# Adjacency loads on another queue, trial sums rearranged, and output tiles opened behind the last search

## The chip, the core and the metric

The kernel runs on one core of a Trainium2 chip. A core has a matrix engine (TensorE, PE in the profile), a vector engine (VectorE, DVE), a scalar engine (ScalarE, ACT), a general-purpose engine (GpSimd, POOL) and a queue that mostly issues DMAs (SyncE, SP). ScalarE and GpSimd can issue DMAs too. Each engine works through its own instructions in order, and they wait for each other by semaphores. The metric is the device time of one execution in microseconds (us).

## The reference, cut to what matters

Two layers over N = 3327 nodes with 256 features. `adj` is a 3327 × 3327 matrix of zeros and ones, about four ones in a row.

```python
# layer 0
Wh  = h @ W
e   = leaky_relu(Wh @ a[:F] + (Wh @ a[F:]).T, 0.2)
att = softmax(where(adj > 0, e, -9e15), axis=1)
x   = layernorm(x + GRU(att @ Wh, x))
# layer 1, two steps; S is adj
R = (S + eye) / rowsum
for n in range(2):
    A  = top_p_attention(Xa, W1, W2, W3)   # softmax of (q k^T); of each row the largest
                                           # probabilities that sum to 0.9 are kept
    Xf = R @ Xf
    Xa = A @ Xa
    Z  = Z + Xf @ U1[n].T + Xa @ U2[n].T
h = X + Z
x = layernorm(x + layernorm(h) * ln_g + ln_b)
```

Everything is in 32-bit floats.

## The kernel before

The rows are cut into 26 tiles of 128 (the last has 127). The work has four stages in the profile: layer 0's projection (0 to about 65 us), layer 0's attention and gates, tile by tile (to about 300), layer 1's first step (about 330 to 960) and second step (about 1000 to 1570), and a tail (to the end at 1846.6).

**Layer 0.** Each tile's adjacency rows are loaded into one of three buffers (`load_adj`, two DMAs of 1248 and 415.5 KB). The vector engine finds the ones of each row (`neighbours`, L819). When it has finished a tile, its number plus three is put on the list `wanted`, since that buffer is free. `advance` counts phases, takes one tile at a time from `wanted`, and issues its load on SP; it also drives the generators `tile(t)`, one opened every 6 phases. Meanwhile `project(t)` computes x W for every tile on PE, ACT copies it out and stores it to a table in DRAM (`whx`). In `tile(t)` GpSimd prepares small vectors (`d1`, `half`, `square`), gathers five times 128 rows of `whx` at the neighbours' numbers (L613), and the other engines turn them into attention and gates. The loads of tiles 1 and 2 go on ACT's queue inside the projection; behind the projection ACT asks for the gates' weights (`whh`, `wih`, 1.54 MB together).

In layer 0 the order on PE, ACT, DVE and GpSimd is the order in which the program is written; in layer 1 the same holds for PE, ACT and DVE, while GpSimd's and SP's orders are chosen by a scheduler.

**Layer 1's step.** For each tile: logits and their exponentials, a search for the threshold that keeps 0.9 of the mass (DVE), a mask, and the product with Xa on PE (`product`, with seven slots into which other work of neighbouring tiles is put).

**Extra tiles.** Rows whose list of candidates was too short in step 2 are put aside (`put_aside_2` stores their data to `left_over` in DRAM at L1531) and searched again in three extra tiles, h0, h1 and h2 (HARD = 3). For each extra tile k: `hard_load` reads the rows' data and gathers their features; `hard_q` computes the query on PE and ACT; `hard_exp` computes the 3327 probabilities. Then an upper bound `top` on the threshold is lowered by trial sums: for f in CUTS = 1/16, 1/4, 1/2, 0.707, 0.841, 0.917, the mass above f × top is summed, and top is multiplied by f when it is less than the wanted mass. A trial sum is done either on ACT (`coarse_bound`: four passes over the probabilities with L1602, and seven small instructions on GpSimd, L1608 to L1617), or on DVE (`bound` with `kept_sum`, L1341: one pass with two inputs from on-chip memory and three small instructions; its comparison at L1632 reads `thr`, which GpSimd makes at L1626). h0 has two cuts on ACT and four on DVE; h1 and h2 have three on each (COARSE = 3). `hard` is the search itself, on DVE (L1644 to L1673 and on); `hard_end` the product and output terms on PE; `hard_store` scatters the rows into the output at L1708.

**Output tiles.** `tile_end(t)`, a generator of eight steps, loads a tile's intermediate rows, transposes them on PE (L1181), sums 16 products and the input on PE (L1440, L1492), copies the sum out on ACT (L1448) and normalizes it twice with statistics on DVE (L1383, L1385), a power on GpSimd (L1386, L1387) and three instructions on ACT.

**The tail's order.** `ends` writes it. DVE's program is the searches of h0, h1, h2, one behind the other. Each `yield` of a search runs `more()`: one step of the queue of the extra tiles' own work (h2's query and exponentials, then the ends of h0, h1, h2), one `tick`, and up to two steps of a coarse bound. A tick opens one new output tile and takes every open one a step further. Since a search has 8 yields and the trial sums in front of h1's and h2's search have three each, there are 30 ticks in the searches.

Of the kernel before, what the change touches and what calls it, by code (L numbers as in the profile page):

```python
# [17 lines left out]
N = 3327  # L18
# [629 lines left out]
class Layer0:  # L648
# [186 lines left out]
    def tile(self, t):  # L835
# [23 lines left out]
        d16 = self.small("d16", f"d16_{t}", dtype=BF16)  # L859
        nc.gpsimd.tensor_copy(d16, d1)  # L860

        nc.gpsimd.tensor_scalar(info[:r, 0:1], info[:r, 0:1], 1.0, None, ALU.max)
        yield from to(2)
        pst = self.ps.tile([P, 512], F32, tag="sm", name=f"pst{t}")
        nc.tensor.matmul(pst[:, 0:1], sh.lower16, d16, start=True, stop=True)

        half = self.small("half", f"half{t}")
        nc.gpsimd.tensor_scalar(half, d1, -0.5, 0.5, ALU.mult, ALU.add)
        square = self.small("square", f"square{t}")
        nc.gpsimd.tensor_scalar(square, d1, d1, 0.25, ALU.mult, ALU.mult)  # L870
        nc.gpsimd.tensor_copy(a[:, :MAXDEG], info[:, :MAXDEG])
        nc.gpsimd.tensor_tensor(b[:, :MAXDEG], info[:, :MAXDEG], a[:, :MAXDEG], ALU.subtract)
        yield from to(4)
# [161 lines left out]
    def run(self):  # L1035
        nc, sh = self.nc, self.sh
        self.load_adj(0, nc.sync)
        parts = self.st.tile([P, 4, DC], F32, tag="parts", name="parts", bufs=1)
        cuts = (0, 8, 16, NT - 2, NT)
        tiles, finding = [], iter(())  # L1040
        found = phase = 0
        self.done, self.searched, self.wanted = 0, False, []
        logits = self.first_logits()

        def find():

            nonlocal finding, found
            if next(finding, True):
                if found < NT:
                    finding = self.neighbours(found)  # L1050
                    found += 1
                    next(finding)
                else:
                    self.searched = True

        def advance(finds):
            nonlocal phase
            for _ in range(finds):
                find()
            if self.wanted and phase > NT - EARLY:  # L1060
                self.load_adj(self.wanted.pop(0), nc.sync)
            if phase % EVERY == 0 and phase // EVERY < NT:
                tiles.append(self.tile(phase // EVERY))
            for g in list(tiles):
                if next(g, True):
                    tiles.remove(g)
                    self.done += 1
            next(logits, None)
            phase += 1

        engines = {
            mybir.EngineType.PE, mybir.EngineType.Activation, mybir.EngineType.DVE, mybir.EngineType.Pool,
        }
        with self.tc.manual_schedule(engines=engines):
            self.weights()
            opened = [self.project(t) for t in range(NT)]
            qk_weights = sh.make_weights(self.work, self.ps)
            pc = self.ps1.tile([1, 512], F32, tag="acc", name="colsum")
            next(opened[0])
            for t in range(NT):  # L1080
                if t + 1 < NT:
                    next(opened[t + 1])
                for _ in opened[t]:
                    pass
                if t in (6, 13):
                    self.load_adj(1 + t // 13, nc.scalar)
                if t in (8, 10):
                    next(qk_weights)
                if t + 1 in cuts:
                    k = cuts.index(t + 1) - 1  # L1090
                    self.column_sums(parts[:, k, :], cuts[k], cuts[k + 1])
                if t - 1 in cuts[1:]:
                    k = cuts.index(t - 1) - 1
                    self.mean_terms(pc, parts[:, k, :], k == 0, False)
                if t == EARLY:
                    self.tell_src(0, EARLY)
                if t >= EARLY:
                    advance(min(1, phase % 2))
                elif t >= EARLY - 9:
                    find()  # L1100
            self.totals(pc, parts[:, 3, :])
            for w, src in zip((self.whh, self.wih), self.gates):
                nc.scalar.dma_start(w, src.rearrange("(c p) d -> p c d", p=P))
            self.tell_src(EARLY, NT)
            while phase < EVERY * NT or tiles:
                advance(FINDS[phase % EVERY] if phase >= 4 * EVERY else 2 if phase >= 16 else 0)
            for _ in logits:
                pass
        full = self.st.tile([P, 3], F32, tag="full", name="full")

        nc.vector.tensor_reduce(full[:, 0:1], self.key.rearrange("p t g e -> p (t g) e")[:, :, 7], AX.X, ALU.max)
        nc.vector.tensor_reduce(full[:, 1:2], self.info[:, :, MAXDEG - 1], AX.X, ALU.max)
        end = self.st.tile([P, NT], F32, tag="e0", name="end", bufs=1)
        nc.vector.scalar_tensor_tensor(end, self.deg, 1.0, self.info[:, :, MAXDEG], ALU.max, ALU.add)
        nc.vector.tensor_reduce(full[:, 2:3], end, AX.X, ALU.max)
        nc.vector.tensor_scalar(full[:, 2:3], full[:, 2:3], -float(EB * P), None, ALU.add)
        nc.vector.tensor_reduce(full[:, 0:1], full, AX.X, ALU.max)
        nc.vector.tensor_scalar(sh.bad[:, 0:1], full[:, 0:1], 0.5, None, ALU.is_gt)
        nc.vector.tensor_scalar(sh.rinv, self.deg, 1.0, None, ALU.add)
        nc.vector.reciprocal(sh.rinv, sh.rinv)  # L1120


class Layer1:
# [432 lines left out]
        )  # L1556

    def hard_q(self, k):
        nc, v = self.nc, self.items[f"h{k}"]
        xt = self.transposed((v.x[:, 0, :],), P, f"q{v.tag}")  # L1560
        pq = self.psm.tile([P, 512], F32, tag="sm", name=f"pq{v.tag}")
        for c in range(DC):
            nc.tensor.matmul(pq[:, :P], self.sh.wq[:, c, :], xt[:, c, :], start=(c == 0), stop=(c == DC - 1))
        v.q = self.work.tile([P, DC, P], F32, tag="xtq", name=f"q{v.tag}")[:, 0, :]
        nc.scalar.copy(v.q, pq[:, :P])

        v.p = (*self.more, self.p[0])[k]
        v.other = (self.l[0][:, :N], self.l[1][:, :N], self.p[1])[k]

        v.top = self.small(f"top{k}", f"top{v.tag}")  # L1570
        nc.scalar.activation(v.top, v.pay[:, 3:4], AF.Exp, bias=v.pay[:, 1:2])
        nc.gpsimd.tensor_scalar(v.top, v.top, 1.0001, None, ALU.mult)
# [14 lines left out]
    def coarse_bound(self, k, cuts, junk):  # L1587
# [6 lines left out]
        for f in cuts:  # L1594
# [21 lines left out]
            nxt = self.small(f"top{k}", f"top{tag}")  # L1616
            nc.gpsimd.tensor_tensor(nxt, up, v.top, ALU.mult)  # L1617
            v.top = nxt
            yield

    def bound(self, k, cuts):
# [122 lines left out]
    def ends(self, bounds):  # L1744


        ends, open_ends, queue = [self.tile_end(t) for t in range(NT)], [], []

        def tick():

            if ends:
                open_ends.append(ends.pop(0))
            for g in list(open_ends):
                if next(g, True):
                    open_ends.remove(g)
# [9 lines left out]
                        break  # L1765

        def start(k):
            self.hard_q(k)
            for pair in self.chunks():
                yield  # L1770
                self.hard_exp(k, pair)
            bounds.append(self.coarse_bound(k, CUTS[:COARSE], self.items[f"h{k}"].other))
# [3 lines left out]
            open_ends.append(self.items[f"h{k}"].end)  # L1776

        queue.append(start(2))
        for k in range(HARD):
            if k:  # L1780
                for _ in bounds[k - 1]:
                    pass
                for _ in self.bound(k, CUTS[COARSE:]):
                    more()
            for _ in self.hard(k):
                more()
            queue.append(end(k))
        while queue or open_ends or ends:
            more()
        for k in range(HARD):  # L1790
# [2 lines left out]
    def run(self):  # L1793
        nc, sh, total = self.nc, self.sh, STEPS * NT
        self.items = {}
        with self.tc.manual_schedule(
# [14 lines left out]
            for i in range(total):  # L1811
# [8 lines left out]
                def slot(g, f, *a):  # L1820
                    slots[g].append(lambda: f(*a))
# [28 lines left out]
                if i == NT + CLOSE + 1:  # L1850
                    slot(0, self.hard_load, 0)
                    slot(0, self.hard_load, 1)
                if i == total - 4:
                    slot(6, self.hard_q, 0)
                if i == total - 2:
                    slot(3, self.hard_q, 1)
                for k, at, first in ((0, total - 3, 0), (1, total - 2, 3)):
                    if i == at:
                        for j, pair in enumerate(self.chunks()):
                            slot(first + j, self.hard_exp, k, pair)  # L1860

                if total - 2 <= i:
                    coarse = self.coarse_bound(0, CUTS[i - total + 2 :][:1], self.l[0][:, :N])
                    for g in (0, 1, 2, 3) if i == total - 2 else (0, 0, 1, 1):
                        slot(g, next, coarse, None)
                for k, pair in enumerate(pairs):
                    slot(2 * k, self.some_logits, i + 2, pair, end)
# [1 line left out]
                    slot(g, next, rest, None)  # L1869
                if i + 1 == total:  # L1870
                    self.put_aside_2(i)
                    bound = self.bound(0, CUTS[2:])
                    bounds = [self.coarse_bound(1, CUTS[:COARSE], self.l[1][:, :N])]
                    for g in (2, 3, 4, 5, 6):
                        slot(g, next, bound, None)
                    for g in (3, 4, 5, 6):
                        slot(g, next, bounds[0], None)
                    slot(5, self.hard_load, 2)
                    for k in range(HARD):
# [101 lines left out]
```

## Time and profile before

The times of three runs are 1852.61, 1852.83 and 1856.24 us.

| | before |
|---|---|
| median of three runs | 1852.83 us |
| the profiled execution | 1848.5 us |
| its span (first to last instruction) | 1846.6 us |
| mean granted TensorE clock | 0.960 |
| trial sums of h0 begin on DVE | 1590.3 us |
| h0's search begins (L1644) | 1607.6 us |
| last search's mask is done on DVE | 1806.1 us |
| last sum of an extra tile is copied out | 1828.75 us |
| first scattered store | 1836.18 us |

A position is the time from the start of the span. A line of a timeline gives start, length, engine, line of the kernel, operation, what is written from what, shapes, and in brackets how long the engine had been idle and what ended the idle time. A line of the waits gives who waited for whom: total us, times, longest.

### The profile page before, as it was taken

What the parts mean: (1) busy time and instruction counts of PE and PEld (TensorE: products, weight loads), DVE (VectorE), ACT (ScalarE), POOL (GpSimd) and SP (SyncE); (2) the same over time, 40 slices, a digit from 0 to 9 for tenths busy, and PEclk for the clock granted to TensorE, in tenths of its full rate; (3) what the DMA queues carried; (4) which work ended last, traced back from release to release, by engine and by line L of the source; (5) the groups of instructions that cost most, each with busy time, mean ns of one, the idle gap of its engine ahead of it and who ended that gap; (6) DMA issues with size and microseconds to landing.
All of it is one profiled execution on the core that took longest, in us unless ns stands there. A gap on an engine that the chain in (4) does not pass through costs nothing. (4 is left out here: it accounts for less than half of the span.)

```text
span 1846.6 us, 27541 instructions
## 1 busy us (share of the span) xinstructions
PE 1654.3 (90%) x8093; PEld 1215.7 (66%) x8093; DVE 1314.9 (71%) x4095; ACT 1030.2 (56%) x2373; POOL 1148.5 (62%) x1908
## 2 busy tenths in 40 slices
PE   6489998969999999999996999999999988679994
PEld 5355555647677777777774777777777656568873
DVE  5788887455555656655546999999999876585872
ACT  3366666646565555555654555555555546677563
POOL 1578777557886666666654556566565572455854
PEclk9799999979999999999998999999999998889997
DMA  9776672222221111111101111111111120122330
GB/s 312 259 251 221 219 218 70 58 63 82 79 58 41 41 41 43 47 47 45 43 26 40 46 50 51 49 55 51 52 49 49 49 63 18 42 76 92 118 98 29
DMA packets 95097, 154.20 MB, mean 84 GB/s; under 512 B 16470, under 2 KB 68173, under 8 KB 94940
## 3 DMA queue, kind: packets, MB, share of 16 engines
q1 hardware_dynamic: 63818, 86.51, 14.4%
q0 software_dynamic: 20384, 53.28, 10.9%
q10 hardware_dynamic: 10738, 12.58, 2.1%
q8 instruction: 66, 1.08, 0.3%
q14 instruction: 91, 0.75, 0.1%
HBM read 124.65 MB, written 27.75 MB: 83 GB/s over the span
## 5 line engine op out<-in xcount | busy, mean ns | idle before, releaser
L1420 PE MATMUL pav<-xa,at 128*128 128x256 f32 (+2 forms) x1352 | 331.8, 390 | 8.8 <-ACT at L1406 8.8
L1406 ACT COPY at<-pt 128x512 f32<-128x512 f32 (+2 forms) x364 | 191.9, 541 | 262.1 <-PE pt L1404 261.4
L1420 PE MATMUL pav<-x,at 128*128 128x256 f32 (+2 forms) x1352 | 325.7, 385 | 7.7 <-ACT at L1406 7.6
L1420 PEld LDWEIGHTS pav<-xa,at 128*128 128x128 f32 (+2 forms) x1352 | 246.5, 192 | 89.8 <-ACT at L1406 43.0
L1420 PEld LDWEIGHTS pav<-x,at 128*128 128x128 f32 (+2 forms) x1352 | 244.4, 190 | 72.5 <-ACT at L1406 28.8
L1200 ACT COPY array<-pl 128x416 f32<-128x416 f32 (+4 forms) x405 | 183.1, 503 | 180.3 <-PE pl L1197 180.2
L1213 DVE MAX8 cand<-array 128x8 f32<-128x167 f32 (+5 forms) x921 | 239.1, 336 | 44.4 <-ACT array L1200 44.4
L613 POOL DMA_INDIRECT g<-xf_rows,edge x130 | 136.4, 1049 | 158.2 <-PE pxf L1366 125.9
L613 POOL DMA_INDIRECT g<-x_rows,edge x130 | 140.4, 1080 | 103.9 <-PE ptq L626 71.0
L1197 PE MATMUL pl<-kT,qT 64*128 64x416 f32 (+4 forms) x810 | 198.0, 560 | 4.5 <-ACT x L1585 2.7
L1305 DVE TENSOR_TENSOR_SCAN before<-e 128x40 f32<-128x40 f32 (+3 forms) x52 | 14.9, 286 | 226.7 <-ACT e L1298 226.7
L1358 POOL TENSOR_SCALAR m<-col,erow 128x128 f32<-128x128 f32 x260 | 162.6, 639 | 14.6 <-PE pxf L1366 8.0
L613 POOL DMA_INDIRECT g<-whx,edge x130 | 141.1, 1085 | 43.9 <-issue 36.1
L1366 PE MATMUL pxf<-g,m 128*128 128x256 f32 (+1 forms) x520 | 133.6, 406 | 15.1 <-POOL m L1358 8.5
L1366 PEld LDWEIGHTS pxf<-g,m 128*128 128x128 f32 (+1 forms) x520 | 98.8, 199 | 69.8 <-issue 41.3
L1231 DVE MAX8 lst<-cand 128x8 f32<-128x160 f32 (+3 forms) x364 | 114.6, 315 | 9.0
L1404 PE MATMUL pt<-ident,array 128*128 128x128 f32 (+1 forms) x676 | 101.1, 276 | 7.1 <-DVE array L1321 7.1
L819 DVE FIND_INDEX8 at<-ones,array 128x8 uint32<-128x840 f32 (+1 forms) x104 | 105.5, 1027 | 0.0
L1404 PE MATMUL pt<-ident,p 128*128 128x128 f32 (+2 forms) x676 | 100.3, 274 | 3.9 <-DVE p L1321 3.9
L1404 PEld LDWEIGHTS pt<-ident,array 128*128 128x128 f32 (+1 forms) x676 | 85.0, 144 | 24.8 <-PE pxf L1366 7.9
L1404 PEld LDWEIGHTS pt<-ident,p 128*128 128x128 f32 (+2 forms) x676 | 84.7, 144 | 21.3 <-PE pxf L1366 7.6
L1321 DVE SCALAR_TENSOR_TENSOR array<-array,t,array 128x3327 f32<-128x3327 f32 x26 | 96.0, 3691 | 0.5
(467 smaller groups left out, 3282.6 us busy)
## 6 DMA issues: line engine op xcount, KB each, us to landing
array<-in_adj_dram SPq DMA_DIRECT2D x23, 1248.0 KB, 6.6
array<-in_adj_dram SPq DMA_DIRECT2D x23, 415.5 KB, 6.7
xf_rows<-xf SPq DMA_DIRECT2D x50, 128.0 KB, 1.7
xa_rows<-xa SPq DMA_DIRECT2D x50, 128.0 KB, 1.7
xfs<-xf_rows SPq DMA_DIRECT2D x50, 128.0 KB, 2.2
whx<-table ACTq DMA_DIRECT2D x25, 129.5 KB, 6.6
x_rows<-x ACTq DMA_DIRECT2D x25, 128.0 KB, 1.7
xb_rows<-xb SPq DMA_DIRECT2D x25, 128.0 KB, 1.7
```

The lines of the kernel that those rows point to most:

```text
L613: self.nc.gpsimd.indirect_dma_start(out=dst[:, b, :], out_offset=None, in_=table[:, :], in_offset=bass.IndirectOffsetOnAxis(ap=self.edge[: ...
L819: nc.vector.max_index(at[:r, g, :], self.ones8[:r], ad[:r, g, :])
L1197: nc.tensor.matmul(pl[:r, :w], q[on], self.sh.kT[on, n, s : s + w], start=True, stop=True)
L1200: nc.scalar.copy(l[:r, h * HALF + s : h * HALF + s + w], pl[:r, :w])
L1213: self.nc.vector.max(cand[:r, g * 8 : g * 8 + 8], src[:r, g * group : min(N, (g + 1) * group)])
L1231: nc.vector.max(lst[:r, k : k + 8], cand[:r])
L1321: nc.vector.scalar_tensor_tensor(v.p[:r], v.l[:r, :N], v.t[:r], v.p[:r], ALU.is_ge, ALU.mult, accum_out=sA[:r])
L1358: nc.gpsimd.tensor_scalar(v.m[:, b, :], sh.col1, sh.erow[:, v.at, b : b + 1], None, ALU.is_equal)
L1366: nc.tensor.matmul(acc[:r, :D], v.m[:, b, :r], v.g[:, b, :], start=(b == 0), stop=(b == EB - 1))
L1404: nc.tensor.transpose(pt[: rows(j), j - j0, :r], v.p[:r, cols(j)], self.ident[:r, :r])
L1406: nc.scalar.copy(at[:, :full, :r], pt[:, :full, :r])
L1420: nc.tensor.matmul(v.acc[: v.r, :D], at[:k, j - 4 * g, : v.r], V[:k, j, :], start=(j == 0), stop=(j == NT - 1))
```

## The change

Four things are changed.

- In `advance`, the loads of tiles 3 to 5 are issued on ACT's queue instead of SP's, at the same place of the program, which on ACT lies just behind the gates' weights. Later tiles stay on SP and no longer wait for phase 14.
- In `tile(t)`, `half` and `square` are computed in front of the first wait step, and the maximum on `info` behind it. On GpSimd this puts them ahead of the previous tile's gather.
- `hard_q` becomes a generator of three steps that are put in three slots. h0 has one cut on ACT (1/16) and five on DVE, in slots 0 to 5 of the last product. h1's first cut on ACT moves from slots 3 to 6 to slots 1 to 4. Each cut on ACT ends with two more empty steps.
- A new output tile is opened only while the number opened is below 0.7 × the number of ticks; behind the last search every tick opens one.

```diff
@@ tile @@
-        nc.gpsimd.tensor_scalar(info[:r, 0:1], info[:r, 0:1], 1.0, None, ALU.max)
-        yield from to(2)
-        pst = self.ps.tile([P, 512], F32, tag="sm", name=f"pst{t}")
-        nc.tensor.matmul(pst[:, 0:1], sh.lower16, d16, start=True, stop=True)
-
         half = self.small("half", f"half{t}")
         nc.gpsimd.tensor_scalar(half, d1, -0.5, 0.5, ALU.mult, ALU.add)
         square = self.small("square", f"square{t}")
         nc.gpsimd.tensor_scalar(square, d1, d1, 0.25, ALU.mult, ALU.mult)
+        yield from to(2)
+        pst = self.ps.tile([P, 512], F32, tag="sm", name=f"pst{t}")
+        nc.tensor.matmul(pst[:, 0:1], sh.lower16, d16, start=True, stop=True)
+
+        nc.gpsimd.tensor_scalar(info[:r, 0:1], info[:r, 0:1], 1.0, None, ALU.max)
         nc.gpsimd.tensor_copy(a[:, :MAXDEG], info[:, :MAXDEG])
@@ advance @@
-            if self.wanted and phase > NT - EARLY:
-                self.load_adj(self.wanted.pop(0), nc.sync)
+            if self.wanted and (self.wanted[0] > 5 or phase > NT - EARLY):
+                t = self.wanted.pop(0)
+                self.load_adj(t, nc.sync if t > 5 else nc.scalar)
@@ hard_q @@
         xt = self.transposed((v.x[:, 0, :],), P, f"q{v.tag}")
+        yield
         pq = self.psm.tile([P, 512], F32, tag="sm", name=f"pq{v.tag}")
...
         nc.scalar.copy(v.q, pq[:, :P])
+        yield
@@ coarse_bound @@
             v.top = nxt
+
+            yield
+            yield
             yield
@@ ends @@
+        ticks = 0
         def tick():
-            if ends:
+            nonlocal ticks
+            ticks += 1
+            if ends and (NT - len(ends) < 0.7 * ticks or not searching):
                 open_ends.append(ends.pop(0))
...
         def start(k):
-            self.hard_q(k)
+            yield from self.hard_q(k)
...
         queue.append(start(2))
+        searching = True
         for k in range(HARD):
...
             queue.append(end(k))
+        searching = False
         while queue or open_ends or ends:
@@ run @@
-                if i == total - 4:
-                    slot(6, self.hard_q, 0)
-                if i == total - 2:
-                    slot(3, self.hard_q, 1)
+                for k, at, first in ((0, total - 4, 4), (1, total - 2, 1)):
+                    if i == at:
+                        q = self.hard_q(k)
+                        for g in range(3):
+                            slot(first + g, next, q, None)
...
-                if total - 2 <= i:
-                    coarse = self.coarse_bound(0, CUTS[i - total + 2 :][:1], self.l[0][:, :N])
-                    for g in (0, 1, 2, 3) if i == total - 2 else (0, 0, 1, 1):
+                if i == total - 2:
+                    coarse = self.coarse_bound(0, CUTS[:1], self.l[0][:, :N])
+                    for g in (0, 1, 2, 3):
                         slot(g, next, coarse, None)
...
-                    bound = self.bound(0, CUTS[2:])
+                    bound = self.bound(0, CUTS[1:])
                     bounds = [self.coarse_bound(1, CUTS[:COARSE], self.l[1][:, :N])]
-                    for g in (2, 3, 4, 5, 6):
+                    for g in (0, 1, 2, 3, 4, 5):
                         slot(g, next, bound, None)
-                    for g in (3, 4, 5, 6):
+                    for g in (1, 2, 3, 4):
                         slot(g, next, bounds[0], None)
```

## The prediction

> **What bounds the kernel now.** First the page's busy shares: TensorE leads overall, but they average over stages.
>
> ```profile
> PE 1654.3 (90%) x8093; PEld 1215.7 (66%) x8093; DVE 1314.9 (71%) x4095; ACT 1030.2 (56%) x2373; POOL 1148.5 (62%) x1908
> ```
>
> Both steps of layer 1 (about 330 to 1570 us) are untouched and cancel. Left are the start and the tail. The tail by windows (columns: length, then busy time of PE, weight loads, DVE, ACT, POOL, each with its count; clock; DMA share; GB/s):
>
> ```profile
> 1570.00:1607.00 37.00, 22.58 (x111) 17.42 (x110) 16.56 (x19) 24.26 (x38) 21.11 (x29) 0.88 0.21 50
> 1607.00:1660.00 53.00, 41.34 (x191) 33.33 (x192) 45.95 (x102) 40.50 (x66) 27.69 (x59) 0.86 0.22 68
> 1660.00:1797.00 137.00, 131.74 (x694) 113.60 (x693) 96.46 (x238) 85.75 (x223) 90.10 (x147) 1.00 0.35 103
> 1797.00:1829.00 32.00, 22.67 (x113) 18.62 (x111) 12.58 (x28) 13.80 (x38) 15.28 (x26) 0.89 0.07 25
> ```
>
> From 1660 to 1797 PE is full (131.7 of 137) while DVE, which runs the three searches one after another, is not: output tiles hold the search back. After that PE waits for the search. DVE's waits over the whole tail say on whom it waits:
>
> ```profile
> DVE bnat L1383 <- ACT qT L1448: 27.1, 7, 10.0
> DVE cndh L1629 <- POOL toph_0.25_16249 L1617: 19.9, 1, 19.9
> DVE bnah L1383 <- ACT xh L1448: 12.3, 2, 7.2
> DVE bnbt L1383 <- POOL qT L1455: 12.2, 5, 8.8
> ```
>
> The statistics of output rows (bnat, bnah, bnbt) stand in DVE's order inside the searches. The 19.9 us end with h0's second coarse cut, seen in POOL's timeline:
>
> ```profile
> 1571.82 2.68 POOL L1531 DMA_INDIRECT left_over<-pay,idx  x1 [3.96 <-issue]
> 1579.08 0.18 POOL L1543 CAST idxh<-payh 128x1 uint32<-128x1 f32 x1 [3.82 <-DMA payh<-left_over]
> 1579.93 0.21 POOL L1626 TENSOR_SCALAR thrh<-payh 128x1 f32<-128x1 f32 x1
> 1580.30 1.17 POOL L1552 DMA_INDIRECT xh<-xa_rows,idxh  x1 [0.16 <-POOL thrh L1626]
> 1589.83 0.19 POOL L1617 TENSOR_TENSOR toph_0.25_16249<-up4h_0.25_16246,toph_0.0625_16115 128x1 f32<-128x1 f32 x1
> ```
>
> At the start, POOL's gathers can begin only once the projection ends, and then nothing but issue stops POOL, about 11.25 us a tile, with the neighbour search on DVE little ahead:
>
> ```profile
> 66.95 0.44 POOL L908 TENSOR_SCALAR edge<-k 128x5 uint32<-128x5 f32 x1 [2.84 <-DVE k L906]
> 68.13 1.21 POOL L613 DMA_INDIRECT g<-whx,edge  x1 [0.74 <-POOL edge L908]
> 69.38 0.21 POOL L868 TENSOR_SCALAR half<-d 128x1 f32<-128x1 f32 x1
> 77.02 0.22 POOL L858 TENSOR_SCALAR d<-deg 128x1 f32<-128x1 f32 x1
> ```
>
> **What the Trainium skill says.** "SBUF — State Buffer", section "Who interferes with whom": a VectorE instruction with two SBUF inputs and a GpSimd instruction that reads SBUF exclude each other for a whole instruction. The trace agrees, with POOL the loser:
>
> ```profile
> 419.36 4.43 POOL L613 DMA_INDIRECT g<-x_rows,edge  x1 [0.16 <-issue]
> ```
>
> This gather began 0.2 us into a DVE pass (L1321, 3.67 us at 419.15) and took 4.43 us; its like take 1.00. The trial sums (L1341) are such passes. "DMA: Bandwidth & Descriptors", section "Issuing engines are not separate DMA queues": the same 16 engines serve every issuer, so another queue gains no bandwidth. In the trace DMA is 95% busy in the first 50 us, whoever issues.
>
> **The adj loads.** Before, SP asks for tile 3 at 25.0 us, as soon as tile 0's buffer is free. Each load is 1.66 MB; three are 5 MB, about 12.8 us at the 390 GB/s at which the DMA view of this stretch peaks. Moved to ACT they stand behind the gate weights (issued at 65.4 and 65.8), so the projection loses their competition: SP has nothing else queued, and ACT's waits behind adj (2.16 us at 36.7, 3.85 at 57.7) and part of the slow matmuls around them go, an estimated 6 to 7 us, and the gates are asked for near 59. But tile 3's rows now land after 1.54 MB of gates and 1.66 of their own: 59.4 + 2.2 + 3.2/0.39 = 69.9, where DVE searches at 67.24 before. DVE has no idle to absorb 2.7 us. POOL needs tile 3's degree at 77.02, 3.4 us after DVE has it, but has only 1.0 us of slack at tile 4. So 2.7 − 1.0 = **+1.7 us** (range −3 to +4). ACT's sixth issue also holds ACT until tile 3 lands; behind it stands the square's input of tile 2 (L875), which before waited 4.51 us for half anyway.
>
> **Half and square** go in front of the gather. ACT's waits for half (64.4 us, 22 times) go, but POOL has the same instructions, and it sets the pace: 0, ±2.
>
> **h0's sums.** ACT loses its second coarse cut, four passes (about 7.6 us); DVE gains one sum (3.68 + 0.67 = 4.36). DVE can begin at 1570.2, as top_0.0625 was there at 1567.6. But the first sum's comparison needs thr (L1626), which still stands behind the store and reload of the left-over rows: 1580.2. Four more sums then end near 1580.7 + 4×4.36 = 1598.2 instead of 1607.56: **−9.4 us**, not the 15.5 that the sums alone would give. Behind this wait DVE has only the sums and the search; nobody else is held. Were the store (2.68 us) itself shut out by the first sum, thr would come up to 2.3 us later; if thr went ahead, up to 6.1 earlier: −3 to −15.5 in all, and I keep the order as built. POOL's gathers for h2 now fall into those sums: the first, which PE needs, still starts before the second sum; the rest get about two per sum and end near 1593 instead of 1588. h1's first cut then is ready near 1602, as before (minus at 1602.75), and its last before DVE comes at 1634: 7 us of margin where there were 16.
>
> **h2's question and the two empty yields** let other work stand between a cut's last pass and the next on ACT, and so may free the 8.50 us that PE waited behind ACT at 1606.95 and the 9.82 at 1654.7. The price is that h2's cuts join two ticks later; DVE asks for them only after h1's search, some 50 us on, so I cost it at nothing; without that cover it is two ticks, about 10 us.
>
> **Fewer tiles in the search.** DVE from 1607.56 to the last search's end at 1806.4: 198.9 us, idle 41.5, work 157.4. The order has 20 full tiles before h2's end instead of 26 and a 21st half open; five or six tiles' statistics leave (four instructions, 1.22 us a tile): about 151.3. Floor of DVE: 1598.2 + 151.3 = 1749.5. Floor of PE: a tile is 5.26 us (1792.31 to 1797.57), 20.5 of them 108; two ends of extra tiles at 21.5; h2's logits 5; begun at 1594: 1750. Two chains of equal length that feed each other don't run at their floor: I leave a third of DVE's idle, 13 us, and take **1763** for the search's end (bounds 1750 and 1791, all idle kept).
>
> **Behind the search.** Before, PE has h2's end alone (1806.17 to 1828.7). Now it has it (21.5) with two tiles inside (10.5), then four output sums and three sets of transposes (20.1): 52.1 us, to 1815. The last tile's rows take what h2's took (1828.75 to 1835.66, less a 0.8 term), 1.2 on ACT, then its store, about 2.7. Only then go the three scattered stores (3.3 us apart; 10.4 from the first to the span's end), which before began just behind h2's rows. 1815 + 6.1 + 1.2 + 2.7 + 10.4 = 1835.5 against 1846.6: **−11.1**. With the start: 1837.2, **−9.4 us**. The profiled execution took 1848.5 for that span; the median is 1852.83, so 1843.4.
>
> **Rivals.** *A, slower:* the search isn't freed. Work behind it costs 72.5 us to the span's end, 40.2 before; with the start's +1.7, the change pays only if the search ends before 1772, which is 34 us earlier; 15.5 come from shorter work, so 19 of 41.5 idle us must go. For it: statistics still stand in DVE's order, and POOL is shut out in the sums. Against: PE, the engine DVE waits for, loses 29 us of work there. All idle kept: 1791 + 72.5 + 1.7 = +18.6, 1871. *B, both chains near their floors* (1750) and the projection's gain is kept (−1): 1828. For it: PE is full at 1.00 clock with waits of only 0.24 to 0.80 us a tile. *C, the order doesn't matter:* search ends at 1772, or the late adj costs 4 and the search 1769: 1853.
>
> **How the numbers follow.** Forecast 0.45 (its own range 1836 to 1849), B 0.19, C 0.12, A 0.24. A difference within 0.2% (3.7 us) can't be told from none. Faster: B and nearly all of the forecast, 0.62; same 0.14, slower 0.24. The range takes B whole and A's nearer half: 1828 to 1864.
>
> **What would show it.** DVE's first comparison waits for thr till about 1580; its last masking pass (L1673) ends at 1755 to 1772; bnat waits fall from 27 to under 12 us; PE works without a break of over 2 us behind the last search; the first scattered store starts 20 us after the last output sum starts to be copied at the latest. In the start: gates asked for near 59, tile 3's search at 69 to 71. I am wrong if the search ends after 1772, or if a cut of h1 or h2 is what DVE waits for.

## The result, and the profile after

The changed kernel took 1866.36 us (median of six runs, 1860.58 to 1871.67) against 1852.38 us before (six runs, 1849.58 to 1856.24): ratio 1.0074, 95% interval 1.0047 to 1.0100. It is slower; the forecast was 0.5% faster, and the measured median lies above the upper end of the range. The profiled execution, the fastest of the six, took 1860.58 us for a span of 1858.7 us, 12.1 us more than the span before.

The tail by windows, cut at this kernel's own marks (h0's sums; to 1650; to the end of the last search; to the last output sum on PE; the rest; columns as before):

```profile
1566.00:1590.00 24.00, 18.11 (x93) 15.20 (x94) 22.59 (x31) 12.90 (x22) 18.28 (x12) 0.90 0.17 34
1590.00:1650.00 60.00, 43.61 (x208) 34.96 (x207) 46.73 (x100) 36.76 (x66) 34.41 (x60) 0.87 0.22 67
1650.00:1779.00 129.00, 111.35 (x550) 94.44 (x548) 96.77 (x221) 76.53 (x182) 81.35 (x131) 0.93 0.29 90
1779.00:1833.00 54.00, 49.98 (x253) 42.66 (x253) 9.17 (x34) 26.54 (x71) 21.86 (x45) 0.97 0.20 62
1833.00:1859.00 26.00, 0.19 (x2) 0.11 (x2) 3.46 (x14) 8.27 (x24) 11.71 (x22) 0.59 0.14 46
```

DVE is busy through h0's sums: the 19.9 us hole is gone, and the wait for `thr` that was forecast there didn't come either. But in the long third window PE is busy for only 111 of 129 us, where it had been full, and DVE still idles for a quarter of it. Then come 54 us in which PE is full (50 us) and DVE has almost nothing (9 us), and 26 in which PE has nothing. Before, 40 us followed the last search; now 79 do.

Who waits, over the tail of the changed kernel; first DVE, then PE:

```profile
DVE bnat L1384 <- ACT qT L1449: 44.4, 14, 9.5
DVE bnah L1384 <- ACT xh L1449: 26.5, 3, 14.7
DVE bnbt L1384 <- POOL qT L1456: 16.2, 11, 3.4
```

```profile
PE pzt L1441 <- ACT xtut L1184: 24.5, 16, 6.9
PE pavh L1421 <- ACT ath L1407: 8.7, 3, 6.4
PE ptxqh L1182 <- DMA xh<-xa_rows,idxh: 5.2, 1, 5.2
```

Some of DVE's waits now lie behind the search, where they are harmless, but 40.3 us are still inside (42.0 before). PE's waits for copied transposes of output tiles rose from 4.7 to 24.5 us. The line before was:

```profile
PE pzt L1440 <- ACT xtut L1183: 4.7, 15, 0.8
```

The end of the kernel, in GpSimd's timeline:

```profile
1843.68 0.55 POOL L1388 TENSOR_TENSOR mvbt<-mvbt,power 127x1 f32<-127x1 f32 x1
1848.76 1.14 POOL L1715 DMA_INDIRECT out_dram<-xh,idxh  x1 [4.53 <-DMA out_dram<-qT]
1852.15 0.98 POOL L1715 DMA_INDIRECT out_dram<-xh,idxh  x1 [2.25 <-DMA out_dram<-xh,idxh]
1854.82 0.97 POOL L1715 DMA_INDIRECT out_dram<-xh,idxh  x1 [1.70 <-DMA out_dram<-xh,idxh]
```

PE's last output sum ended at 1832.9; the last tile's rows needed until 1844, its store another 4.5 us, and only then came the three scattered stores.

The start, in the timelines of DVE, ACT and GpSimd:

```profile
66.75 0.09 DVE L819 MATCH_VALUE_LOAD at<-ones,array 128x8 f32 x1 [7.97 <-DMA array<-in_adj_dram]
67.19 0.26 ACT L875 ACTIVATE mid<-pst,half 128x1 f32<-128x1 f32 x1 [10.64 <-DMA array<-in_adj_dram]
59.58 1.21 POOL L613 DMA_INDIRECT g<-whx,edge  x1 [0.74 <-POOL edge L908]
77.65 0.43 POOL L908 TENSOR_SCALAR edge<-k 128x5 uint32<-128x5 f32 x1 [2.04 <-DVE k L906]
```

The projection ended 8.5 us earlier (first gather 59.58 instead of 68.13). DVE then waited 8 us for tile 3 and ACT 10.6 for its own blocked issue, and the second tile's edges came at 77.65, where they had come at 77.74.

All runs below are compared by marks on DVE, counted from the put-aside of the last tile but one, so that differences in earlier stages drop out (us, worked out from the timelines). "Searched" is the end of each search, "behind" the time from the end of the last search to the end of the span, "to the end" the time from the mark to the end of the span, and "waits" are DVE's between the start of h0's search and the end of the last.

| kernel | last put-aside | h0's search begins | h0, h1, h2 searched | behind | to the end | waits |
|---|---|---|---|---|---|---|
| before | +18.0 | +55.6 | +90.5, +176.9, +254.4 | 40.3 | 294.7 | 42.0 |
| changed | +14.4 | +37.7 | +73.2, +155.4, +227.3 | 79.3 | 306.6 | 40.3 |
| open every tick | +14.4 | +37.6 | +76.5, +175.9, +255.8 | 41.2 | 297.0 | 59.0 |
| open at 0.85 | +14.4 | +37.7 | +76.5, +168.6, +245.1 | 55.5 | 300.6 | 53.7 |
| changed, no empty steps | +14.4 | +37.7 | +80.5, +162.9, +235.1 | 77.8 | 312.9 | 49.1 |
| only late opening | +18.0 | +55.6 | +91.0, +170.1, +243.0 | 77.9 | 320.9 | 39.4 |
| only sums | +14.4 | +37.6 | +76.4, +175.9, +256.0 | 40.8 | 296.8 | 59.3 |
| sums, h2 later | +14.4 | +37.7 | +77.7, +180.0, +262.4 | 41.8 | 304.2 | 65.6 |
| sums, no empty steps | +14.4 | +37.7 | +80.1, +173.0, +253.5 | 40.7 | 294.1 | 57.6 |
| only split query | +14.4 | +54.2 | +89.0, +175.6, +254.6 | 41.7 | 296.3 | 43.2 |
| split and empty steps | +14.4 | +54.3 | +89.8, +181.5, +261.4 | 41.6 | 303.1 | 48.2 |
| half the tile work | +18.1 | +55.6 | +90.9, +165.0, +237.7 | 41.8 | 279.6 | 26.2 |

### The profile page after: what moved, and what is told of

Its sections match the earlier page's. It is cut to its first block, busy times and chain, and to the rows that moved or that the text cites. A ratio compares the mean times of both kernels' runs of the same rounds, so it can differ in the third digit from the quotient of the medians.

```text
span 1858.7 us, 27527 instructions
## 1 busy us (share of the span) xinstructions
PE 1657.1 (89%) x8093; PEld 1218.6 (66%) x8093; DVE 1320.5 (71%) x4100; ACT 1023.1 (55%) x2365; POOL 1158.3 (62%) x1899
## 3 DMA queue, kind: packets, MB, share of 16 engines
q0 software_dynamic: 20384, 53.28, 10.6%
## 4 chain that ended last, share of the span: by engine, by line
PE 41%; DVE 26%; POOL 14%; issue 8%; ACT 6%; DMA 3%; ACTq 0%; POOLq 0%; another core or an unknown queue 0%; SPq 0%; DVEq 0%
PE pav L1421 16%; POOL g L613 6%; DVE cand L1214 5%; PE pl L1198 5%; DVE array L1336 5%; DVE cand L1234 4%; PE pxf L1367 3%; DVE lst L1232 3%; PE pt L1405 3%; PE pzt L1441 3%; DVE array L1322 2%; PE pavh L1421 2%; DVE p L1322 2%; DMA array<-in_adj_dram 1%; PE acc L940 1%
## 5 line engine op out<-in xcount | busy, mean ns | idle before, releaser
L1421 PEld LDWEIGHTS pav<-xa,at 128*128 128x128 f32 (+2 forms) x1352 | 245.1, 191 | 86.5 <-ACT at L1407 39.6
L613 POOL DMA_INDIRECT g<-x_rows,edge x130 | 136.5, 1050 | 104.5 <-PE ptq L626 71.6
```

Of the source, the lines that this page charges most:

```text
L613: self.nc.gpsimd.indirect_dma_start(out=dst[:, b, :], out_offset=None, in_=table[:, :], in_offset=bass.IndirectOffsetOnAxis(ap=self.edge[: ...
L1421: nc.tensor.matmul(v.acc[: v.r, :D], at[:k, j - 4 * g, : v.r], V[:k, j, :], start=(j == 0), stop=(j == NT - 1))
```

## The experiments

Every ratio below is to the kernel before as it was timed beside that experiment (medians between 1849.2 and 1851.9 us), with its 95% interval. The times of different experiments are therefore compared by their ratios. The letters of theories and rivals are explained where they first stand.

**The opening put back in the changed kernel.**

```diff
-            if ends and (NT - len(ends) < 0.7 * ticks or not searching):
+            if ends:
```

> The changed kernel with one line put back: a new output tile is opened on every tick, as before. Theory L (the late opening is the loss): in the changed kernel the last search ended 27 us earlier, but 17.9 of that came from h0's earlier start and only 9.8 from the two later searches, while the work behind the search grew from 40 to 79 us. Put back, the search ends near 1789 and 40 us follow: span near 1829, 17 us under before. Rival P (GpSimd held by h0's sums delays h2's data and everything queued behind it on ScalarE): the loss stays, time near 1860.

Measured: 1852.77 us, ratio to before 1.0017 (1.0006 to 1.0027). In the changed kernel the late opening is most of the loss: 0.57 of 0.74%. But the 17 us that theory L promised did not come: h0's search began 18 us earlier than before and the last one ended no earlier (+255.8 against +254.4). What DVE gained at the front it lost in waits (59.0 against 42.0).

**The late opening alone, put into the kernel before** (the `ticks` and `searching` lines of the change only).

> The kernel before with only the opening at 0.7 per tick. Theory L: search ends some 10 us earlier (near 1796), 79 us follow: span near 1875, 28 us slower. Rival P: it costs nothing by itself, within 5 us of before.

1873.79 us, ratio 1.0140 (1.0112 to 1.0169): 26 us slower, where theory L had 28. The search ended 11.4 us earlier and 37.6 us were added behind it. Rival P, to which the late opening costs nothing by itself, falls. Fewer tiles in the search left DVE with 39.4 us of waits, where it had 42.0: this is the premise of the forecast, tried alone.

**Both layer 0 edits alone**, then each alone (the `advance` lines, and the move of `half` and `square`).

> The kernel before with only the layer 0 edits (adj loads of tiles 3 to 5 on ScalarE's queue, half and square in front of the gather). In the changed kernel the put-aside of the last tile came 3.6 us earlier than before. If this is theirs, 3 to 4 us faster; on record I had reckoned 1.7 us slower.

1851.38 us, ratio 1.0013 (1.0004 to 1.0023): slower, the earlier put-aside was not theirs.

> The kernel before with only the adj loads of tiles 3 to 5 on ScalarE's queue; half and square stay. Both together made it 0.13% slower (2.4 us). If the late landing of tile 3 is the cause, as I had reckoned, this alone is 2 us slower; if the half and square are, this alone is 0 to 2 us faster.

1850.55 us, ratio 1.0000 (0.9988 to 1.0012). The adj loads are worth nothing in either direction: the waits for tile 3 are there too (DVE's three waits for adj sum to 10.0 us, the longest 8.0), and eat exactly what the projection gained.

> The kernel before with only half and square in front of the gather. Both layer 0 edits together were 0.13% slower, the adj loads alone 0.00%. If the effects add, this is 1 to 4 us slower; on record I had 0 with 2 us to both sides.

1853.08 us, ratio 1.0014 (1.0006 to 1.0023). So this edit is the slower one of the two. One tile of layer 0 later on, from one edge calculation to the next, on GpSimd (lines between are left out); before, and then this run:

```profile
141.46 0.20 POOL L908 TENSOR_SCALAR edge<-k 128x5 uint32<-128x5 f32 x1
143.12 0.21 POOL L868 TENSOR_SCALAR half<-d 128x1 f32<-128x1 f32 x1
143.29 0.31 POOL L870 TENSOR_SCALAR square<-d 128x1 f32<-128x1 f32 x1
152.43 0.21 POOL L862 TENSOR_SCALAR info<-info 128x1 f32<-128x1 f32 x1
152.72 0.20 POOL L908 TENSOR_SCALAR edge<-k 128x5 uint32<-128x5 f32 x1
```

```profile
143.82 0.20 POOL L908 TENSOR_SCALAR edge<-k 128x5 uint32<-128x5 f32 x1
145.48 0.26 POOL L870 TENSOR_SCALAR info<-info 128x1 f32<-128x1 f32 x1
154.72 0.19 POOL L863 TENSOR_SCALAR half<-d 128x1 f32<-128x1 f32 x1
154.88 0.27 POOL L865 TENSOR_SCALAR square<-d 128x1 f32<-128x1 f32 x1
155.23 0.20 POOL L908 TENSOR_SCALAR edge<-k 128x5 uint32<-128x5 f32 x1
```

From one tile to the next the same instructions take 11.41 us instead of 11.26, and nearly the same holds for the tiles around this one: two small ones now stand in front of the gather, 0.51 us from the first to the edge calculation, where the one on `info` took 0.29; what stands behind it, with that one, shrank by only 0.07 (10.90 for 10.97). GpSimd sets the pace of this stage; 0.15 us in some 24 tiles are 3.6 us, and 2.6 were measured. Why an order costs more than another with the same instructions isn't settled.

**The rearranged sums alone.** The changed kernel without the layer 0 edits and with every tick opening.

> The kernel before with only the rearranged trial sums (layer 0 and the opening of tiles as before). Theory L: h0's search starts 14 us earlier and nothing is lost behind: 10 to 14 us faster. Rival P: 5 us slower or more, because the data of h2 comes late.

1849.64 us, ratio 1.0006 (0.9996 to 1.0016): neither theory. h0's search starts 18 us earlier, the last ends 1.6 us later than before, and DVE's waits grew from 42.0 to 59.3 us.

**How many tiles to leave.**

```diff
-            if ends and (NT - len(ends) < 0.7 * ticks or not searching):
+            if ends and (NT - len(ends) < 0.85 * ticks or not searching):
```

> The changed kernel with 0.85 in place of 0.7: about three output tiles are left behind the last search instead of six. Theory W (PE is full in the tail, so a tile moved behind the search saves the search about its own PE time and costs it again behind, and the last tile's rows add a fixed end): from the two profiles, six tiles shortened the search by 28.5 us (4.8 each) and lengthened what follows by 38 (5.26 each and some 6.5 fixed). Three tiles: search 14 earlier, 16 and 6.5 more behind: 8 us slower than with every tick, near 1861. A rival (only the tiles that h2's end can't cover cost): three fit beside it, 0 to −5 us, near 1850.

1859.87 us, ratio 1.0035 (1.0019 to 1.0050). In this run two output sums come behind the last search, in the changed kernel six, with every tick none. Against every tick, two shorten the search by 10.7 us and add 14.3 behind it; six shorten it by 28.5 and add 38.1. So here a tile saves about 5 us in the search and costs 6.4 to 7.2 behind. On the kernel before it saved less: six tiles 11.4 us, 1.9 each, at 6.3 behind. The exchange loses at both numbers tried; with two tiles by 3.6 us in the profiles and 0.18% in the ratios, which is at the edge of what their intervals tell apart, and less than the 8 us of theory W.

**Is PE what DVE waits for?** The kernel before without the second step's half of each output tile.

```diff
-            self.transposed((a[:r, D : 2 * D], xa2[:r]), r, f"vt{t}"),
```

> The kernel before, which leaves out the second step's half of each output tile's sum (two of four transposes, 8 of 16 products): 2.3 us of PE time a tile, 61 us in all; the output is without these terms. Theory W: PE is the bound of the search's time, DVE's 41.5 us of waits for output rows mostly go, search ends 25 to 35 us earlier, and so does the kernel: near 1820. Rival Q (ScalarE's order, with its waits for GpSimd, holds the rows): DVE keeps over 30 us of its waits and less than 10 us are gained.

1839.01 us, ratio 0.9925 (0.9898 to 0.9951): the estimated 61 us of PE work bring 14 (PE's busy time in the tail fell by 45 us, from 218.3 to 173.7). DVE keeps 26 of its 42 us of waits, and PE, with so much less to do, waits longer for the copies of output tiles (29.2 us, before 4.7):

```profile
PE pzt L1440 <- ACT xtut L1183: 29.2, 15, 5.3
PE pth L1404 <- DVE array L1672: 10.4, 1, 10.4
PE plh L1581 <- ACT array L1584: 10.1, 2, 9.1
PE pavh L1420 <- ACT ath L1406: 8.0, 2, 5.3
```

Both theories fall by their own numbers (W wanted 25 to 35 us, Q under 10 with over 30 us of waits kept). PE's work is a part of the bound and not the bound: with nearly half of it gone 16 of 42 us of waits go, and waits of up to 5.3 us appear behind ScalarE's copies. The run doesn't separate PE from ScalarE: the line left out also takes a copy of about 0.59 us a tile from ScalarE, some 15 us in all. And TensorE's granted clock over the tail was lower in it (0.85 against 0.92), so it may understate what the work costs.

**h2's query three ticks later** (three `yield`s in front of it in `start`, on the kernel with only the sums).

> The kernel with only the rearranged sums, and h2's query three ticks later, so that PE and ScalarE don't stand behind h2's gather, which GpSimd does late because the sums shut it out (gathers of 3.9 to 4.3 us instead of 1.0; PE waited 5.2 us for it). If that wait is on the path: 4 to 6 us faster than with only the sums, near 1845. If not, or if h2's cuts come late for DVE: no change, or slower.

1858.27 us, ratio to before 1.0039 (1.0026 to 1.0051), so 0.33% slower than without the delay. ScalarE now stood 16.1 us (7.8 without it) before h1's second cut, waiting for GpSimd's `minus`, and PE 15.6 us behind ScalarE. A longer wait took the place of the one for the gather, so that this run doesn't tell what those 5.2 us are worth; it shows only that a later query isn't the way to save them.

**The sums taken apart.** Four kernels: only the query in three slots; the same with the two empty steps; all of the sums' part but the empty steps; and the changed kernel without them. The last two leave the empty steps out so:

```diff
             v.top = nxt
-
-            yield
-            yield
             yield
```

> The kernel before with only the extra tiles' query in three slots. In every run with it the last put-aside came 14.4 us after the one before instead of 18.05. PE is the bound of what follows, so the 3.6 us should reach the end: 3 to 4 us faster. If the search, not PE, sets the end: no change.

1846.94 us, ratio 0.9986 (0.9977 to 0.9995): faster, about as expected.

> The same and the two empty steps behind each ScalarE cut; h0 keeps two cuts on ScalarE and four sums on DVE, in the slots of before. Theory M (the loss inside the sums' part comes from the cut moved to DVE, whose sums shut GpSimd out and make h2's data late): without it the empty steps let PE off its 8.5 us wait, 6 to 10 us faster than before. Theory Y (the empty steps themselves do it: they push h2's ScalarE cuts in between the output tiles of h1's search, where PE waits for copies behind them): no faster than the split alone, and PE waits of 3 to 8 us for copies of output tiles.

1855.08 us, ratio 1.0025 (1.0013 to 1.0036). Theory M falls and Y holds: the empty steps cost 0.39% here, and PE's waits for copied transposes are 22.4 us (5.8 with the split alone). The one long wait of PE behind a ScalarE cut, 11.4 us with the split alone, did go, as the prediction hoped; the new waits outweigh it:

```profile
PE pzt L1440 <- ACT xtut L1183: 22.4, 15, 8.4
```

> The kernel with only the rearranged sums, without the two empty steps: query in three slots, one cut of h0 moved from ScalarE to DVE, h1's first cut two slots earlier. The empty steps alone took the split from 0.14% faster to 0.25% slower (7 us). If they cost the same here, this is 0.3% faster than before (6 us, near 1845): the moved cut then brings some 3 us. If the moved cut itself is the loss (GpSimd shut out by the sums), no faster than the split alone, or slower.

1846.62 us, ratio 0.9984 (0.9974 to 0.9993). Beside the split alone the moved cut (with h1's first cut two slots earlier, which wasn't tried apart) brings nothing that can be told: h0's search starts 16.5 us earlier, the last ends 1.1 us earlier, and DVE's waits are 14 us longer. These two are the fastest kernels of the study that compute everything, and beat both before and changed.

> The changed kernel without the two empty steps. If what kept the search waiting in spite of fewer tiles is ScalarE's cuts between the output tiles, PE's 24.5 us of waits for copied transposes fall to about 17 and the time by 5 to 8 us, near 1859; the six tiles behind the search still make it slower than before. If not, no change.

1866.12 us, ratio 1.0087 (1.0068 to 1.0106): a miss. PE's waits for those copies fell to 13.8 us, but ScalarE's wait in front of h1's second cut grew to 11.4 us (from 7.8) with PE 13.1 us behind it, and the search ended later (+235.1, with them +227.3). With the late opening no cost of the empty steps can be told; the two intervals overlap.

## Why the prediction was wrong, point by point

Its main account can be closed in numbers. The search was to end at 1763 and ended at 1779.4 (16.4 later); 72.5 us were to follow and 79.3 did (6.8 more); the 1.7 us that were charged to the start are inside these positions. 16.4 + 6.8 − 1.7 = 21.5, which is 1858.7 − 1837.2. The 16.4 us have parts of both signs: h0's search began 8.5 us earlier than reckoned (1589.7 for 1598.2), DVE's work in the searches took 1.9 us less (149.4 for 151.3), and 40.3 us of idle stood in them for 13.5. The unforeseen early start hid a third of the error.

- **The step that failed is "fewer tiles in the search": "I leave a third of DVE's idle, 13 us".** It rested on "PE, the engine DVE waits for". DVE kept 40.3 us. The late opening alone shows that this isn't the doing of the sums: there DVE kept 39.4 of 42.0. The half-work run shows the premise wrong in size: with nearly half of PE's work on the tiles gone, and ScalarE's copies for it, only 16 of 42 us went. On top of the rearranged sums the late opening did cut the waits, from 59.0 us to 40.3, but that is no more than the sums had added (42.0 to 59.0): the prediction put both gains into one sum, from an idle time that one of them raised. What holds the rows up seems to be a ring of four engines, each in its fixed order; the changed kernel's timelines show a turn of it:

```profile
1628.38 3.87 DVE L1342 SCALAR_TENSOR_TENSOR array<-x,cndh 128x3327 f32<-128x3327 f32 x1
1628.85 3.98 POOL L1456 TENSOR_TENSOR qT<-qT 128x256 f32<-128x256 f32 x1
1633.78 0.29 ACT L1395 ACTIVATE shiftat<-shiftat,mvat 128x1 f32<-128x1 f32 x1 [5.66 <-POOL mvat L1388]
1638.97 1.65 PE L1421 MATMUL pavh<-xa,ath 128*128 128x256 f32 x3 [6.36 <-ACT ath L1407]
1648.52 0.43 DVE L1384 BATCH_NORM_STATS2 bnat<-qT 128x6 f32<-128x256 f32 x1 [7.72 <-ACT qT L1449]
1649.25 0.19 POOL L1387 TENSOR_SCALAR mvat<-mvat 128x1 f32<-128x1 f32 x1 [6.06 <-DVE cndh L1636]
```

  DVE's sum at 1628.38 (3.87 us) holds a GpSimd addition that takes 0.72 when free; ScalarE, which needs GpSimd's power behind it, idles 5.66 us, has two passes of h2's cut (1634.87 to 1638.35) next in its order, and so comes late to the copies of PE's transposes; PE idles 6.36, the tile's sum is late, DVE waits 7.72 for its row, and GpSimd then waits for DVE. Where the ring turns on ScalarE's cuts and GpSimd's powers instead of PE's sums, fewer tiles on PE would not speed it up. That the ring is the cause in the whole search is read from the waits and not shown by a run; the runs show that PE's work alone is not, and that the empty steps add to DVE's waits only where tiles open on each tick (43.2 to 48.2, 57.6 to 59.3).
- **h0's sums: −9.4 us expected, with a wait for thr to 1580.** That row was h2's thr; h0's had been made near 1478, and no such wait came. The search began 17.9 us earlier; the split query alone gave 1.4 of them, the moved cut with it the rest. But I carried the gain to the end of the search, and in every kernel with the moved cut that opens tiles on each tick it was given back as waits: 57.6 to 65.6 us instead of 42.0. Part of it is kept only where the late opening also stands (searched at +227.3, with the late opening alone +243.0), and there the opening adds more behind the search than it saves.
- **The empty steps** I took for a gain at no price. With every tick opening they cost 0.22 to 0.39% (the former is the sums with and without them). The guess that "other work" would stand between the cuts was right; by the waits, ScalarE's copies for PE came to stand behind cuts.
- **Behind the search.** PE's part was right: 53.5 us against 52.1. The end was not: from PE's last sum to the span's end 25.8 us instead of 20.4, because, by the timelines, the last tile's rows share the closing ticks with those of the other late tiles (11.3 us to its last power, 6.1 expected) and the store took 4.5 with the last instruction on ScalarE, 3.9 expected.
- **Rival A** named what failed and nearly its size (1871 us for 1866): the idle is kept, and the point of 1772 from which it decides was passed by 7 us. I gave it 0.24 because I read PE's full window as the reason for DVE's idle. A check was at hand: taking work from PE shortens DVE's waits only if ScalarE, which copies for both, has room; and behind the start of h0's search there stand five coarse cuts of four passes in ScalarE's order (1.8 us a pass, in the changed kernel) among these copies.
- **The adj loads:** the step was right in kind, not in size. Gates were asked for at 56.8 (59 expected), tile 3's search began at 66.75 (69.9 expected), and the gain was eaten as forecast: 0.00%, reckoned as 1.7 us. The rate of 390 GB/s was set low as the peak: slices of the DMA view of the kernel before between 20 and 70 us reach 420. **Half and square:** 2.6 us slower, just outside the 2 that I allowed (its interval begins at 1.1); I counted the instructions and not their places, in a stage where I had myself called GpSimd the pace.
- **GpSimd shut out by the sums** held as the Trainium skill has it ("SBUF — State Buffer", section "Who interferes with whom"): three of h2's gathers in the sums took 3.9 to 4.3 us instead of 1.0, and all of them had ended at 1598.2 (1593 expected). The same section infers that one kind of pass with two such inputs, `tensor_tensor`, leaves the making of a DMA's descriptors alone; the passes here are another kind (`scalar_tensor_tensor`), and the gathers were held. PE's 5.2 us wait for the first of them I had not reckoned with.

The parts as measured: adj 0.00, half and square +0.14, split −0.14, moved cut −0.02, empty steps +0.22, late opening +0.57, together +0.77 against +0.74%. That they add up is no proof of the account: the last four are steps from one kernel to the next, so only the layer 0 parts could have missed. And the size of a part depends on what stands beside it: the late opening costs 1.40% alone and 0.57 here.

## What to carry to other kernels

A full engine in front of another engine's waits is no proof that its work is the bound: when nearly half of that work was taken away here, most of the wait stayed, and an experiment that leaves work out is a cheap way to see it. Work moved behind the end of a critical chain must save more in the chain than it costs behind it, its own serial end included: here 2 to 5 us were saved and 6.3 to 7.2 spent a tile. An earlier start of a chain that reads other engines' results in its middle counts only if those come earlier too. And two savings that draw on the same idle time can't be added.

## What the runs showed that was not expected

- The late opening left DVE's waits as they were when it stood alone (42.0 to 39.4 us) and cut them by 18.7 us when the sums had raised them.
- The order of the same small GpSimd instructions around a gather was worth 0.15 us a tile and 0.14% of the kernel.
- An edit that splits one burst of dependent steps over three slots (the query) shortened the two last steps in which it stands by 2.5 and 3.7 us, yet 0.14% of the whole, some 2.6 us, was left of it at the end.
